# Attention outputs of two batches at once, and their products with W_out in seven: a two-layer graph attention kernel

## The chip, the cores and the metric

The kernel runs on one core of a Trainium2 chip. The metric is device time in microseconds, measured from outside the kernel; the median of three runs of the kernel before is 2986.15 us (2981.69 to 2986.96).

A core has five engines with instruction queues of their own: TensorE (PE; its weight loads are listed apart as PEld), VectorE (DVE), ScalarE (ACT), GpSimd (POOL) and SyncE (SP), which here only issues DMAs. Each engine works through its queue in order and waits on semaphores for the others. SBUF is the working memory, PSUM [...] is where TensorE writes.

## The reference

The input is x of 128 batches x 128 nodes x 512 features, fp32, and an adjacency mask of 128 x 128 per batch. Two layers follow each other. With LN the layer norm without scale and shift:

```
layer 0:  q, k, v = x Wq, x Wk, x Wv                 (4 heads of 64)
          P = softmax(where(adj, q k^T / 8, -max))
          h = LN(x + concat(P v) Wo + bo)
layer 1:  q, k, v = (LN(h) * gamma + beta) Wqkv^T    (8 heads of 64)
          P = softmax(where(adj | eye, q k^T / 8, -1e9))
          out = LN(h + concat(P v) Wout^T + b_out)
```

## The kernel before

All arithmetic is fp32. Two batches make a group (G = 2), so there are NG = 64 groups. The program is a software pipeline written out by hand: `step(s)` (L531) issues the work of several groups in a fixed order, and that order is the order of each engine's queue; nothing reorders it. In step s stand, among others, layer 0's q, k, v products of group s, layer 0's scores of group s - 1, layer 1's q and k products of group s - 2, and layer 1's scores and v products of group s - 3. A step has two halves, one for each batch of its groups (k = 2s and 2s + 1).

*Products in seven.* The q, k, v products take a group's two batches and two halves of the features as a 2 x 2 block matrix and form seven half-size products in place of eight (Winograd's form of Strassen's method). `sums` (L257, four additions on GpSimd at L266) makes the sums of the left side; the sums of the weights are made once. Products 1, 6, 7 and 4 accumulate one after the other in one PSUM bank ("a"), 5 and 3 in another ("f"), 2 in a third ("c"). After each product its bank is read, by ScalarE (1, 5, 6, 4) or by VectorE (2, 3, 7), before the next product of that bank may write. `product` (matmuls at L304; reads at L330, L332, L335) does so for layer 1, `product_0` (L361; L371, L373, L376) for layer 0. Below, "qk product 5" or "v product 4" are these.

*Attention.* `scores` (L386) multiplies q with k into rotating PSUM banks (pool ps_mm, five banks), GpSimd fills the target with the masked value (L410), VectorE copies the scores where the mask allows it (L412) and takes the row maximum (L415); for layer 1 it first joins the mask with the unit matrix (L407). ScalarE takes exponentials and their sums, one instruction per head (L424). `normalised` (L427) takes reciprocals on VectorE and multiplies on GpSimd (L433). To transpose the probabilities, `blocks` (L436) transposes 32 x 32 blocks on VectorE (L448), and two rounds of DMA through a scratch in HBM (`put` L198, `fetch` L204) move the blocks. `attend` (L458) multiplies them with v and ScalarE copies the result out (L474), batch by batch.

*Output and normalisation.* `residual` (L487) multiplies one batch's attention output with W_out, 512 columns at a time: two matmuls in layer 0, four in layer 1 (L493), each recorded as two instructions. VectorE adds the residual (L499), to which `addend` (L476) had added the bias on GpSimd (L484), and takes mean and variance (L501, L503); GpSimd forms the roots (L506 to L517); `norms` (L522) normalises on VectorE (L524), called later by `flush`. Layer 0's result h is then turned in the same way as the probabilities: `turn` (L208) transposes on VectorE (L214) and puts it, `arrive` (L219) fetches it, `finish` (L245) brings it in order on ScalarE and applies gamma and beta (L252), and `sums` follows. Layer 0's input x takes the same path through `in_order` (L235, ScalarE at L241). ScalarE rescales h (L483) to the residual of layer 1, since layer 1's norm is applied together with layer 0's.

SP issues every DMA in program order: loads (L72, L73), puts, fetches and outputs (L528).

Of the kernel before, what the change touches and what calls it, by code (L numbers as in the profile page):

```python
# [17 lines left out]
P = 128  # L18
# [9 lines left out]
def kernel(ctx: ExitStack, tc: tile.TileContext, x, adj, wq, wk, wv, wo, bo,  # L28
# [13 lines left out]
    four = ctx.enter_context(tc.tile_pool(name="four", bufs=4))  # L42
    dram = ctx.enter_context(tc.tile_pool(name="dram", bufs=2, space=bass.MemoryType.DRAM))
    ps_mm = ctx.enter_context(tc.tile_pool(name="ps_mm", bufs=5, space=PSUM))
# [9 lines left out]
    later, waiting = [], []  # L54
# [5 lines left out]
    def exponentials(left=0):  # L60
        while len(waiting) > left:
            waiting.pop(0)()


    X, M = {}, {}

    def load(g):
        if g >= NG:
            return
        X[g] = four.tile([P, G, E], F32, tag="x", name=f"x_{g}")  # L70
        M[g] = four.tile([P, G, N], U8, tag="m", bufs=6, name=f"m_{g}")
        nc.sync.dma_start(X[g], x[g * G:(g + 1) * G].rearrange("b n e -> n b e"))  # L72
        nc.sync.dma_start(M[g], adj[g * G:(g + 1) * G].rearrange("b i j -> i b j"))  # L73
# [8 lines left out]
    mhalf = const.tile([P, 2], F32, name="mhalf")  # L82
# [25 lines left out]

    spare = []
    for tag, n in (("qk1", 4), ("v1", 2), ("xT1", 2), ("xs1", 2)):  # L110
        rows_n = one.tile([P, n, E], F32, tag=tag, name=f"raw_{tag}")
        spare.extend(rows_n[:, i] for i in range(n))

    def load_transposed(dst, src, name, scaled=0):
        rows, cols = src.shape
        raws = []
        for r in range(rows // P):
            if not spare:
                raw = three.tile([P, cols], F32, tag="h", bufs=7, name=f"{name}_{r}")
            else:  # L120
                raw = spare.pop(0)
            nc.sync.dma_start(raw, src[r * P:(r + 1) * P, :])
            raws.append(raw)
# [36 lines left out]
    def weight_sums():  # L160
        for w, ws in ((w1qk, wsqk), (w1v, wsv)):
            for c in range(KH):
# [6 lines left out]
                t2, t3, t4 = ws[:, 0, c], ws[:, 1, c], ws[:, 2, c]  # L169
                nc.vector.tensor_sub(t3, b22, b12)  # L170
                nc.vector.tensor_sub(b12, b12, b11)
                nc.vector.tensor_sub(t2, b22, b12)
                nc.vector.tensor_sub(t4, b21, t2)

    def weight_sums_0():
        b11, b12, b21, b22 = (w0[:, c:c + KH, h].rearrange("p c t f -> p c (t f)")
                              for c in (0, KH) for h in range(2))
        t2, t3, t4 = (ws0[:, i].rearrange("p c t f -> p c (t f)") for i in range(3))
# [4 lines left out]

    weight_sums_0()
    load_transposed(w1, w_qkv, "w_qkv", scaled=INNER[1])
    setup.append(turn_gamma_beta)
    load_transposed(wo1, w_out, "w_out")
    setup.append(weight_sums)

    WO = (wo0, wo1)  # L190
    RATIO, H, XT, QK, V, QKV = {}, {}, {}, {}, {}, {}
# [14 lines left out]
    TURNED, SCR, RAW = {}, {}, {}  # L206

    def turn(l, g, b):  # L208
        if not 0 <= g < NG:
            return  # L210
        if b == 0:
            TURNED[l] = one.tile([P, 4, G * KC * 32], F32, tag=f"turned{l}", name=f"turned{l}_{g}")
        src = X[g][:, b] if l == 0 else H[g, b]
        nc.vector.transpose(TURNED[l].rearrange("p a (b c i) -> p a b c i", b=G, c=KC)[:, :, b],  # L214
                            src.rearrange("p (c a i) -> p a c i", a=4, i=32))
        if b == G - 1:
            SCR[l] = put(TURNED[l], f"scr{l}_{g}")

    def arrive(l, g):  # L219
        if not 0 <= g < NG:  # L220
            return
        RAW[l] = one.tile([P, 4, G, KC, 32], F32, tag=f"raw{l}", name=f"raw{l}_{g}")
        fetch(RAW[l].rearrange("p a b c i -> p a (b c i)"), SCR[l])

    def first_transposed():
        xT = XT[0, 0] = one.tile([P, KC, T], F32, tag="xT0", name="xT0_0")
        for b in range(G):
            pt = mm_tile(f"xt_{b}")
            for c in range(KC):
                nc.tensor.transpose(pt[:, c * N:(c + 1) * N], X[0][:, b, c * P:(c + 1) * P], ident)  # L230
# [26 lines left out]
    def sums(l, g):  # L257
        xT = XT[l, g]
        xs = one.tile([P, 4, KH, N], F32, tag=f"xs{l}", name=f"xs{l}_{g}")
        a = xT.rearrange("p (h c) (b n) -> p b h c n", h=2, b=2)  # L260
# [6 lines left out]
        XS[l, g] = xs  # L267
# [362 lines left out]
```

## Time and profile before

| What | Value |
|---|---|
| median of three runs | 2986.15 us (2981.69 to 2986.96) |
| the profiled execution | 2984.46 us |
| its span, first to last instruction | 2982.7 us |
| mean granted TensorE clock | 0.994 |
| TensorE busy | 2920.0 us (98%) |
| VectorE, ScalarE, GpSimd busy | 1854.0 (62%), 1334.2 (45%), 1567.4 us (53%) |
| DMA | 414 MB, 139 GB/s in the mean |
| W_out matmuls (L493) | 1536 instructions, 713.2 us busy |

The profile is of one execution. A line of the timeline gives start (from the span's start), length, engine, source line, operation, written tile <- read tiles, shapes and count; a bracket tells how long the engine idled before it and what ended that. The chain of waits is followed backwards from the last instruction: each piece is what its successor waited for. A busy share is a mean over the whole span and doesn't say whether an engine was late at the moment at which it was wanted.

### The profile page before, as it was taken

The numbers are of one execution on the slowest core, as the hardware profiler recorded it, in microseconds if no ns is written. First come the engines' busy times: TensorE is split into PE (matmuls) and PEld (weight loads), VectorE is DVE, ScalarE is ACT, GpSimd is POOL, SyncE is SP. The second block draws the span as 40 slices with busy tenths as digits, with TensorE's granted clock in tenths as the row PEclk, the third lists the DMA queues.
The fourth block names the chain that finished last, engine by engine and source line by source line (L and its number), as shares of the span: only waits on it lengthen the run. The fifth ranks groups of instructions, "written<-read, shape, count | busy, mean of one in ns | idle before, by whom it ended". The sixth has DMA issues, their size and how long they took to land.

```text
span 2982.7 us, 59421 instructions
## 1 busy us (share of the span) xinstructions
PE 2920.0 (98%) x22089; PEld 2402.9 (81%) x22089; DVE 1854.0 (62%) x3291; ACT 1334.2 (45%) x4619; POOL 1567.4 (53%) x2055
## 2 busy tenths in 40 slices
PE   6899999999999999999999999999999999999997
PEld 5788888888888888888888888888888888888865
DVE  4466666666666666666656666666666666666654
ACT  2344444444444444444544444444444444444442
POOL 2455545545545555555555555455455455455543
PEclk8999999999999999999999999999999999999999
DMA  5454544544544544544544545545445445445332
GB/s 170 123 149 129 150 141 127 161 136 124 165 135 125 165 136 127 160 134 134 156 132 140 150 131 147 146 129 153 141 126 161 137 122 168 133 125 163 118 100 89
DMA packets 249136, 414.42 MB, mean 139 GB/s; under 512 B 41608, under 2 KB 181392, under 8 KB 248848
## 3 DMA queue, kind: packets, MB, share of 16 engines
q1 hardware_dynamic: 248848, 410.62, 46.3%
q8 instruction: 175, 2.87, 0.4%
q14 instruction: 113, 0.93, 0.1%
HBM read 209.72 MB, written 200.80 MB: 138 GB/s over the span
## 4 chain that ended last, share of the span: by engine, by line
PE 96%; DVE 1%; DMA 1%; ACT 1%; issue 0%; POOL 0%; SPq 0%; POOLq 0%; DVEq 0%; ACTq 0%
PE o L493 22%; PE qka L304 15%; PE a L361 12%; PE qkf L304 8%; PE va L304 8%; PE sc L400 6%; PE av L471 6%; PE f L361 6%; PE qkc L304 4%; PE vf L304 4%; PE c L361 3%; PE vc L304 2%; ACT sm L424 1%; DMA scrp<-turned 0%; DMA pT<-scrp 0%
## 5 line engine op out<-in xcount | busy, mean ns | idle before, releaser
L424 ACT ACTIVATE sm<-sm,nmax 128x128 f32<-128x128 f32 x1536 | 595.2, 389 | 618.6 <-DVE nmax L415 604.9
L493 PE MATMUL o<-wo,aT 128*128 128x512 f32 x1536 | 713.2, 600 | 10.0 <-ACT aT L474 10.0
L506 POOL TENSOR_SCALAR ve<-mv 128x1 f32<-128x1 f32 x256 | 57.0, 223 | 1133.0 <-DVE rec L432 798.8
L493 PEld LDWEIGHTS o<-wo,aT 128*128 128x128 f32 x1536 | 278.3, 191 | 269.3 <-issue 246.8
L433 POOL TENSOR_TENSOR sm<-sm,rec 128x512 f32<-128x512 f32 (+1 forms) x256 | 397.0, 1561 | 171.9 <-DVE rec L432 171.9
L412 DVE COPY_PREDICATED sm<-m,sc 128x512 f32<-128x512 uint8 (+1 forms) x512 | 271.0, 581 | 29.1 <-POOL sm L410 7.0
L424 ACT ACTIVATION_READ_ACCUMULATOR sm<-sm,nmax 128x1 f32 x1536 | 288.0, 187 | 0.0
L448 DVE STREAM_TRANSPOSE turned<-sm 128x512 f32<-128x512 f32 (+1 forms) x256 | 246.0, 965 | 45.0 <-POOL sm L433 45.0
L304 PE MATMUL qkf<-xs,w 128*128 128x128 f32 x2048 | 249.9, 275 | 0.1
L304 PE MATMUL qka<-xs,wsqk 128*128 128x128 f32 x2048 | 249.6, 275 | 0.0
L415 DVE TENSOR_REDUCE nmax<-sm 128x4 f32<-128x512 f32 (+1 forms) x256 | 244.0, 953 | 8.8
L304 PEld LDWEIGHTS qkf<-xs,w 128*128 128x128 f32 x2048 | 239.0, 192 | 0.6 <-POOL xs L266 0.4
L304 PEld LDWEIGHTS qka<-xs,wsqk 128*128 128x128 f32 x2048 | 239.0, 192 | 0.0
L524 DVE TENSOR_SCALAR h<-h,mv,rstd 128x512 f32<-128x512 f32 x128 | 70.0, 547 | 265.0 <-POOL rstd L513 265.0
L432 DVE RECIPROCAL rec<-total 128x4 f32<-128x4 f32 (+1 forms) x256 | 44.7, 175 | 296.6 <-ACT sm L424 296.6
L266 POOL TENSOR_TENSOR xs<-xT 128x256 f32<-128x256 f32 x256 | 186.0, 727 | 34.4 <-PE w_qkvt L129 14.5
L410 POOL MEMSET sm<- 128x512 f32 (+1 forms) x256 | 181.1, 735 | 1.4 <-DVE turned L448 1.3
L330 ACT COPY ev<-va 128x256 f32<-128x256 f32 x128 | 47.6, 372 | 298.7 <-PE va L304 298.7
L513 POOL TENSOR_TENSOR rstd<-ve,mhalf 128x2 f32<-128x2 f32 (+1 forms) x256 | 165.9, 648 | 21.3
L330 ACT COPY eqk<-qka 128x512 f32<-128x512 f32 x128 | 75.1, 587 | 214.4 <-PE qka L304 214.4
L484 POOL TENSOR_TENSOR h<-h,bias 128x512 f32<-128x512 f32 x128 | 162.7, 1271 | 7.0 <-ACT h L483 6.9
L484 POOL TENSOR_TENSOR x<-x,bias 128x512 f32<-128x512 f32 x128 | 162.2, 1267 | 0.0
(122 smaller groups left out, 5825.5 us busy)
## 6 DMA issues: line engine op xcount, KB each, us to landing
scrp<-turned SPq DMA_DIRECT2D x124, 768.0 KB, 3.3
pT<-scrp SPq DMA_DIRECT2D x496, 192.0 KB, 4.0
scr<-turned SPq DMA_DIRECT2D x127, 512.0 KB, 2.7
raw<-scr SPq DMA_DIRECT2D x508, 128.0 KB, 3.0
x<-in_x_dram SPq DMA_DIRECT2D x64, 512.0 KB, 4.2
out_dram<-y SPq DMA_DIRECT2D x128, 256.0 KB, 2.0
m<-in_adj_dram SPq DMA_DIRECT2D x64, 32.0 KB, 4.0
scrp<-turned SPq DMA_DIRECT2D x4, 512.0 KB, 3.2
```

Source lines behind the costliest of these rows:

```text
L266: nc.gpsimd.tensor_tensor(o, a0, a1, op=op)
L304: nc.tensor.matmul(o, lhsT, rhs, start=first and n == 0, stop=n == len(todo) - 1, skip_group_check=True)
L361: nc.tensor.matmul(acc[:, t * P:(t + 1) * P], lhsT, rhs, start=first and n == 0, stop=n == len(todo) - 1, skip_group_check=True)
L400: nc.tensor.matmul(ps[h % 2][:, h // 2, :], q_, k_, start=True, stop=True)
L410: nc.gpsimd.memset(sm, (NEG0, NEG1)[l])
L412: nc.vector.copy_predicated(sm[:, s], mask[:, None, :].to_broadcast([P, K, N]), ps[s][:, :K, :])
L415: nc.vector.tensor_reduce(nmax, sm, AX.X, ALU.max, negate=True)
L424: nc.scalar.activation(sm[:, s, k, :], sm[:, s, k, :], AF.Exp, bias=nmax[:, s, k:k + 1], accum_out=total[:, s, k:k + 1])
L433: nc.gpsimd.tensor_tensor(sm, sm, rec[:, :, :, None].to_broadcast([P, 2, K, N]), op=ALU.mult)
L448: nc.vector.transpose(t[:, :, lo:hi, :], sm)
L484: nc.gpsimd.tensor_tensor(xin, xin, (bias0, bias1)[l], op=ALU.add)
L493: nc.tensor.matmul(pm, aT[:, c * P:(c + 1) * P], WO[l][:, c, :], start=(c == 0), stop=(c == nk - 1))
```

## The change

Layer 0's and layer 1's products with W_out are formed in seven for the two batches of a group, as the q, k, v products are; each product is added by VectorE straight from PSUM into its quarter of the residual R, which takes the place of x, h and y in one buffer of six. The left side's sums are four more GpSimd additions per layer (`out_sums`). `attend` runs once a step for both batches, one step later than before for layer 1. Means, roots and normalisations are made for both batches of a group; layer 1's normalisation moves from VectorE to ScalarE, output and load are one DMA each per group. The mask is joined with the unit matrix once per group. The rotating PSUM banks become four, and layer 0's second accumulating bank gets one of its own. `step` is written anew, with NG + 4 steps. In the first products of its second half, an output addition stands between the two layers' masks.

The core of the diff; the old bodies of the functions are shown above.

```diff
-    four = ctx.enter_context(tc.tile_pool(name="four", bufs=4))
+    six = ctx.enter_context(tc.tile_pool(name="six", bufs=6))
-    ps_mm = ctx.enter_context(tc.tile_pool(name="ps_mm", bufs=5, space=PSUM))
+    ps_mm = ctx.enter_context(tc.tile_pool(name="ps_mm", bufs=4, space=PSUM))
...
+    def turn(l, g):
+        if not 0 <= g < NG:
+            return
+        t = one.tile([P, 4, G * KC * 32], F32, tag="turned_in", name=f"turned{l}_{g}")
+        for b in range(G):
+            nc.vector.transpose(t.rearrange("p a (b c i) -> p a b c i", b=G, c=KC)[:, :, b],
+                                R[g][:, b].rearrange("p (c a i) -> p a c i", a=4, i=32))
+        SCR[l] = put(t, f"scr{l}_{g}")
+    def out_product(l, g, *which):
+        if not 0 <= g < NG:
+            return
+        aT, so = AT[l, g], SO[l, g]
+        hk = INNER[l] // P // 2
+        w, ws = WO[l], WSO[l]
+        EH = E // 2
+        for i in which:
+            left = {1: aT[:, 0, :hk], 2: aT[:, 0, hk:], 3: so[:, 3], 4: aT[:, 1, hk:], 5: so[:, 0],
+                    6: so[:, 1], 7: so[:, 2]}[i]
+            right = {1: w[:, :hk, :EH], 2: w[:, hk:, :EH], 3: w[:, hk:, EH:], 4: ws[:, 2],
+                     5: w[:, :hk, EH:], 6: ws[:, 0], 7: ws[:, 1]}[i]
+            bank, first = INTO[i]
+            if first and bank == "c":
+                ACC["o", bank] = mm_tile(f"oc{l}_{g}")
+            elif first:
+                ACC["o", bank] = ps_st.tile([P, 512], F32, tag=(bank, f"{bank}0")[l], name=f"o{bank}{l}_{g}")
+            acc = ACC["o", bank][:, :EH]
+            for c in range(hk):
+                nc.tensor.matmul(acc, left[:, c], right[:, c], start=first and c == 0, stop=c == hk - 1,
+                                 skip_group_check=True)
+            b, h = {1: (0, 0), 2: (0, 0), 6: (0, 1), 3: (0, 1), 5: (1, 1), 7: (1, 1), 4: (1, 0)}[i]
+            part = R[g][:, b, h * EH:(h + 1) * EH]
+            nc.vector.tensor_add(part, acc, part)
...
+    def with_self(g):
+        if 0 <= g < NG:
+            nc.vector.tensor_tensor(M[g], M[g], eye[:, None, :].to_broadcast([P, G, N]), op=ALU.max)
...
+    def attend(s):
+        for l, g in ((0, s - 2), (1, s - 4)):
+            if not 0 <= g < NG:
+                continue
+            K = HEADS[l] // 2
+            aT = AT[l, g] = one.tile([P, G, K, N], F32, tag=f"aT{l}", name=f"aT{l}_{g}")
+            for b in range(G):
+                pT = PT.pop((l, g, b))
+                if l == 1 or b == 0:
+                    pm = mm_tile(f"av{l}_{g}_{b}").rearrange("p (k n) -> p k n", n=N)
+                for h in range(HEADS[l]):
+                    i, kk = h % 2, h // 2
+                    o = pm[i * D:(i + 1) * D, (b * K if l == 0 else 0) + kk, :]
+                    v = (QKV[g][:, b, kk, 2, i * D:(i + 1) * D] if l == 0
+                         else V[1, g][:, b, h * D:(h + 1) * D])
+                    nc.tensor.matmul(o.rearrange("p (a r) -> p a r", r=32), v, pT[:, :, i * K + kk, :],
+                                     start=True, stop=True)
+                if l == 1:
+                    nc.scalar.copy(aT[:, b], pm)
+                elif b == G - 1:
+                    nc.scalar.copy(aT.rearrange("p b k n -> p (b k) n"), pm)
+    def out_sums(l, g):
+        if not 0 <= g < NG:
+            return
+        K = HEADS[l] // 2
+        so = SO[l, g] = one.tile([P, 4, K // 2, N], F32, tag=("so", "xs0")[l], name=f"so{l}_{g}")
+        halves_sums(so, AT[l, g].rearrange("p b (h c) n -> p b h c n", h=2))
+    def addend(l, g):
+        if not 0 <= g < NG:
+            return
+        if l == 1:
+            for b in range(G):
+                nc.scalar.activation(R[g][:, b], R[g][:, b], AF.Copy, scale=RATIO[g][:, b:b + 1])
+        nc.gpsimd.tensor_tensor(R[g], R[g], (bias0, bias1)[l][:, None, :].to_broadcast([P, G, E]),
+                                op=ALU.add)
+    def stats(l, g, b):
+        if not 0 <= g < NG:
+            return
+        if b == 0:
+            MV[l, g] = two.tile([P, G, nc.vector.BN_AGGR_DIM], F32, tag="mv", name=f"mv{l}_{g}")
+        st = three.tile([P, nc.vector.BN_STATS_DIM], F32, tag="st", name="st")
+        nc.vector.bn_stats(st, R[g][:, b])
+        nc.vector.bn_aggr(MV[l, g][:, b], st)
+        if b == G - 1:
+            roots(l, g)
+    def roots(l, g):
+        mv = MV[l, g]
+        n = 2 - l
+        ve = two.tile([P, 2, G], F32, tag="ve", name=f"ve{l}_{g}")
+        nc.gpsimd.tensor_scalar_add(ve[:, 0], mv[:, :, 1], EPS)
+        if l == 0:
+            nc.gpsimd.tensor_scalar(ve[:, 1], mv[:, :, 1], 1.0 + EPS, EPS * EPS, op0=ALU.mult,
+                                    op1=ALU.add)
+        root = two.tile([P, 2, G], F32, tag="root", name=f"root{l}_{g}")
+        nc.gpsimd.tensor_tensor(root[:, :n].rearrange("p i b -> p (i b)"),
+                                ve[:, :n].rearrange("p i b -> p (i b)"), mhalf[:, :n * G], op=ALU.pow)
+        if l == 0:
+            ratio = RATIO[g] = three.tile([P, G], F32, tag="ratio", bufs=5, name=f"ratio_{g}")
+            nc.gpsimd.tensor_tensor(ratio, ve[:, 1], root[:, 1], op=ALU.mult)
+            nc.gpsimd.tensor_tensor(ratio, ratio, root[:, 0], op=ALU.mult)
+            later.append(lambda: norms_0(g, mv, root))
+        else:
+            shift = two.tile([P, G], F32, tag="shift", name=f"shift_{g}")
+            nc.gpsimd.tensor_tensor(shift, mv[:, :, 0], root[:, 0], op=ALU.mult)
+            nc.gpsimd.tensor_scalar_mul(shift, shift, -1.0)
+            later.append(lambda: norms_1(g, shift, root))
+    def norms_0(g, mv, root):
+        for b in range(G):
+            nc.vector.tensor_scalar(R[g][:, b], R[g][:, b], mv[:, b, 0:1], root[:, 1, b:b + 1],
+                                    op0=ALU.subtract, op1=ALU.mult)
+    def norms_1(g, shift, root):
+        for b in range(G):
+            nc.scalar.activation(R[g][:, b], R[g][:, b], AF.Identity, bias=shift[:, b:b + 1],
+                                 scale=root[:, 0, b:b + 1])
+        nc.sync.dma_start(out[g * G:(g + 1) * G].rearrange("b n e -> n b e"), R[g])
...
+        k = 2 * s
+        if s:
+            load(s + 1)
+        made = scores(k)
+        masked(made, 0)
+        masked(made, 1)
+        exps(0, k)
+        addend(0, s - 2)
+        with_self(s - 2)
+        p("qk", 4, g=s - 3)
+        product_0(s, 1)
+        attend(s)
+        exps(1, k)
+        out_sums(0, s - 2)
+        product_0(s, 5)
+        p("", g=-1)
+        product_0(s, 2)
+        addend(1, s - 4)
+        p("", g=-1)
+        out_product(0, s - 2, 1, 5, 2)
+        normalised(k)
+        out_product(0, s - 2, 6)
+        product_0(s, 6)
+        p("", g=-1)
+        out_product(0, s - 2, 3)
+        stats(0, s - 2, 0)
+        out_product(0, s - 2, 7)
+        product_0(s, 3)
+        p("", g=-1)
+        out_product(0, s - 2, 4)
+        product_0(s, 7)
+        stats(0, s - 2, 1)
+        p("v", 1, 5, g=s - 3)
+        blocks(k)
+        product_0(s, 4)
+        p("v", 2, g=s - 3)
+        flush()
+        turn(1, s - 2)
+        arrive(1, s - 2)
+        probs_arrive(k)
+        k += 1
+        made = scores(k)
+        masked(made, 0)
+        p("v", 6, g=s - 3)
+        out_sums(1, s - 4)
+        out_product(1, s - 4, 1)
+        exps(0, k)
+        masked(made, 1)
+        p("v", 3, g=s - 3)
+        exps(1, k)
+        out_product(1, s - 4, 5, 2)
+        p("v", 7, g=s - 3)
+        out_product(1, s - 4, 6)
+        p("v", 4, g=s - 3)
+        normalised(k)
+        finish(s - 2)
+        turn(0, s + 1)
+        blocks(k)
+        out_product(1, s - 4, 3)
+        stats(1, s - 4, 0)
+        out_product(1, s - 4, 7)
+        arrive(0, s + 1)
+        probs_arrive(k)
+        p("qk", 1)
+        p("qk", 5)
+        out_product(1, s - 4, 4)
+        stats(1, s - 4, 1)
+        p("qk", 2)
+        p("qk", 6)
+        in_order(s + 1)
+        flush()
+        p("qk", 3, 7)
     first_transposed()
-    for s in range(NG + 3):
+    for s in range(NG + 4):
         step(s)
```

## The prediction

> **What bounds the kernel now.** I read the page first, then the chain of waits over one step, then VectorE, ScalarE and GpSimd in the same stretch. Page and chain:
>
> ```profile
> span 2982.7 us, 59421 instructions
> PE 2920.0 (98%) x22089; PEld 2402.9 (81%) x22089; DVE 1854.0 (62%) x3291; ACT 1334.2 (45%) x4619; POOL 1567.4 (53%) x2055
> ```
> ```profile
> 1454.99 1.54 PE sc L400 x24
> 1456.53 3.63 PE o L493 x8
> ...
> 1470.43 1.72 PE o L493 x4
> 1472.15 0.86 PE va L304 x4
> ...
> 1478.01 1.06 PE va L304 x4
> 1479.07 3.43 PE o L493 x8
> ...
> 1486.36 1.72 PE o L493 x4
> ...
> 1498.35 1.79 PE qka L304 x16
> 1500.14 1.54 PE sc L400 x24
> ```
>
> The chain is TensorE alone. A step (two batches) lasts 1500.14 - 1454.99 = 45.15 us, and 60 full steps run from 145.6 to 2854. The other 2982.7 - 60 x 45.15 = 274 us are filling and draining. The output products take 3.63 + 1.72 + 3.43 + 1.72 = 10.50 us of a step; the rest takes 34.65. A pass of 512 columns costs 3.43/8 = 0.429 us, one of 256 costs 0.86/4 = 0.216. Going to or from the 64-row score matmuls costs about 0.2 (va: 1.06 instead of 0.86).
>
> VectorE around the second half's scores, then one GpSimd and one ScalarE line:
>
> ```profile
> 1475.23 0.55 DVE L524 TENSOR_SCALAR h<-h,mv,rstd 128x512 f32<-128x512 f32 x1 [1.40 <-POOL rstd L513]
> 1475.81 0.71 DVE L214 STREAM_TRANSPOSE turned<-h 128x512 f32<-128x512 f32 x1
> 1476.44 0.39 DVE L335 TENSOR_TENSOR v<-vc,ev 128x256 f32<-128x256 f32 x1
> 1476.75 0.41 DVE L335 TENSOR_TENSOR v<-vf,ev 128x256 f32<-128x256 f32 x1
> 1477.21 0.78 DVE L412 COPY_PREDICATED sm<-m,sc 128x256 f32<-128x256 uint8 x2
> 1478.02 0.69 DVE L415 TENSOR_REDUCE nmax<-sm 128x4 f32<-128x512 f32 x1
> ...
> 1479.04 1.34 DVE L412 COPY_PREDICATED sm<-m,sc 128x512 f32<-128x512 uint8 x2
> 1480.41 1.22 DVE L415 TENSOR_REDUCE nmax<-sm 128x8 f32<-128x1024 f32 x1
> ...
> 1485.18 1.25 DVE L524 TENSOR_SCALAR y<-y,mv,rstd 128x512 f32<-128x512 f32 x1
> ```
> ```profile
> 1485.11 3.08 POOL L433 TENSOR_TENSOR sm<-sm,rec 128x512 f32<-128x512 f32 x2
> ```
> ```profile
> 1486.44 2.07 ACT L252 ACTIVATE xT<-raw,gb 128x256 f32<-128x256 f32 x4
> ```
>
> VectorE runs in order; start to start gives what each costs the queue: 0.31 for a 256-wide addition from PSUM, 0.81 + 0.61 and 1.37 + 1.14 for the two layers' masks and maxima, 0.63 for a transpose. It keeps up now because the second half of a step (from 1476.47) has room: only one normalising and one turning stand there ahead of the scores.
>
> [...] here 256 columns from PSUM last 0.41, 512 last 0.69, so splitting costs. [...] the trace agrees (1.25 at 1485.18 behind a GpSimd multiplication, 0.51 when ahead of one). [...] the change puts products 1, 6, 7, 4 into one bank, each after VectorE has read the last.
>
> **The change, part by part, per step.**
> *Output products.* 24 passes of 512 become 42 of 256: 14 in layer 0, 28 in layer 1. 42 x 0.216 = 9.07, saving 1.43. One visit to the attention outputs instead of two saves one switch (0.2), and scores are now followed by short products that pay it. TensorE without waits: 34.65 + 9.05 = 43.7 us.
> *VectorE.* Four 512-wide additions (4 x 0.69) go, 14 of 256 (14 x 0.41 = 5.7) come; two scalings (2 x 0.89) move to ScalarE at 0.73; a mask operation of two goes. Net +1 us, about 30 of 44: not full, but see below.
> *GpSimd.* Eight half sums more: four of 256 (4 x 0.73), four of 128, which the trace lacks; the line through 0.73 (256) and 1.27 (512) gives 0.46, bounds 0.37 (half of 0.73) and 0.73. Bias additions of 1024 by the same line: 2.4, bounds 2.1 (the 1024 multiplication) and 2 x 1.27. Power over four values: 0.58 (one), 0.72 (two), so 1.0; bounds 0.72 and 1.44. Net about +3, under 28 of 44.
> *Moved.* The bringing in order of the next group's xT (L241, two copies, then four sums at L266) goes behind layer 1's qk product 6: copies end 1.8 before the step does, the sums 1.4 into the next, and the two memsets queued behind them on GpSimd (0.52 + 0.95) make the first masks 1.0 late. Covered: the exponentials that follow are wanted only behind the attention outputs at 8.5; without that cover it would be 1.0 a step. The two scalings now on ScalarE (1.4) run at the step's end under qk products 3 and 7 (3.6). The mask operation (0.28 before, 0.28 to 0.56 now) stands where VectorE idles until layer 0's q, k, v product 2. Layer 0's normalising and turning now come together, both batches, on VectorE right behind the last addition of v (product 2) and ahead of the second scores. On SP the put (L198) and four fetches (L204) move with them, past no slow wait; in before put to last landing is 8.2 to 9.8 us behind other transfers, 2.7 + 1.3 + 2.8 = 6.8 without, which I take. Output and load are one DMA each per group, hidden: the load, issued at a step's head, lands in 4.2 after the output's 2 and is turned 30 us later. Four rotating PSUM banks instead of five: the last score bank waits for that v addition, 0.1.
>
> *The walk.* Hand-overs cost about 0.1 (layer 0's f ends at 1470.43 on the chain, its addition starts at 1470.54). TensorE in the new order: scores 1.54, qk product 4 1.99, attention 3.12, seven layer 0 q, k, v products 7 x 1.34, seven output products 7 x 0.43, v's products 1, 5 and 2 3 x 0.86: their end is 21.6 after the step's start. On the way layer 0's output product 4 waits for output product 7's addition, queued behind the first batch's statistics (0.69 + 0.18): output product 3 ends at 14.3, its addition, the statistics and that addition at 16.1, TensorE is ready at 15.9: wait 0.3. GpSimd: ScalarE rescales the residual behind the eight exponentials (until 13.3: attention copies end at 8.5, exponentials 3.09, one copy, two rescalings), then bias 2.4, multiplications 1.04 + 2.08 to 18.9, roots to 21: just in time.
>
> Now from that end (V): VectorE v addition to +0.4; two normalisings 0.92, plus 0.5 for GpSimd's sums (bounds 0 and 1.5, two whole 0.73 sums), +1.8; two transposes +3.1; layer 0 masks and maxima +4.5; one output addition +4.8; layer 1 masks and maxima, maxima ready +7.4; three additions +8.2; v product 7's addition +8.65. TensorE wants v product 4, same bank, at 1.54 + 0.2 + 7 x 0.86 = +7.76: it gets it at +8.75, and all behind it waits 1.0.
> Behind that addition stand on VectorE product 6's addition, the reciprocals, two transposes of x and those of the probabilities; none of these is wanted by TensorE before qk product 5.
> ScalarE: eight exponentials 3.09 (eight took 1462.46 to 1465.55 in before) from +7.5, v copy, four xT activations (L252): the second chunk at +11.95, the last +12.95. GpSimd sum +13.75. So layer 1's qk product 5, due at +12.13, starts at +13.85: 1.7 late, the wait of 1.0 included. What is late next: layer 1's output product 4 waits for product 7's addition, behind transposes of probabilities (GpSimd done +13.0), product 3's addition and statistics: +16.0 against +15.65: 0.35.
>
> Sum: 43.7 + 0.3 + 1.7 + 0.35 = 46.1 us, 0.9 over before. 60 x 46.1 = 2766. Filling and draining: one more step (layer 1's attention a step later), but no attention in the second step; 274 becomes 280 (260 to 300). Span 3046. The profiled execution took 1.8 more than its span and the median is 1.7 above it: **3050 us**.
>
> **Rivals.**
> *A, faster: TensorE stays the bound.* The chain v addition, masks, exponentials, xT, sum fits into TensorE's 12.1 us up to product 5 or nearly. For it: no engine's busy time is near 44. Against it: its parts sum to 13.85 even when nothing collides (13.35). It decides once waits are under 1.35 a step ((2983 - 280)/60 = 45.05). With 0.5 of waits: 60 x 44.2 + 280 + 4 = 2936; with none 2906.
> *B, slower still, one collision fully paid.* Both normalisings wait for a GpSimd sum each (+1.0), or the fetch takes 9.8 as before behind the probabilities' put instead of 6.8: it lands at +13 where ScalarE wants it at +10.9 (+2). 47.1 to 48.1: 3110 to 3170.
> *C, saving and waits cancel:* 45.05, 2980 to 2992.
> *D, the change doesn't do what it says:* 14 short groups each lose 0.1 at their head and the saving is gone. Against: va, vf, vc, equally short, follow each other at 0.86.
>
> **How the numbers follow.** Likeliest 0.52: 45.6 to 46.9, 3020 to 3098, its own range. A 0.24, spread from 2906 to 2980; B 0.18, from 3098 to 3170; C (with D) 0.06. Range 2945 to 3120: 0.1 of A and 0.1 of B stay outside. Measurement tells 0.2%, 6 us. Faster 0.24, same 0.06, slower 0.70.
>
> **What would show it.** The distance between steps on the chain, 46.1; va L308 waiting for VectorE once a step, near 1 us; qkf waiting for GpSimd's or qka for ScalarE's xT; VectorE normalisings longer than 0.55; TensorE busy share under 96%; output passes at 0.216. Wrong if the step is 44 with no wait on va, if the fetch decides, or if a pass of 256 costs more than 0.22.

## The result and the profile after

| | before | after |
|---|---|---|
| median of four runs, us | 2984.86 (2981.69 to 2986.96) | 3069.73 (3068.78 to 3070.35) |
| span of the profiled execution, us | 2982.7 | 3066.9 |
| one full step, us: median (mean of 60) | 45.14 (45.15) | 46.02 (46.05) |
| filling and draining, us: span less 60 mean steps | 274 | 304 |

The kernel before has one run more here than above, so its median differs a little. The changed kernel is slower: the ratio is 1.0285, with a 95% interval of 1.0267 to 1.0303. The medians stand 2.8 us above the span here and 2.2 us before. First the head of the page of the changed kernel:

```profile
span 3066.9 us, 62670 instructions
PE 2925.4 (95%) x23241; PEld 2645.0 (86%) x23241; DVE 1896.0 (62%) x3747; ACT 1432.8 (47%) x4683; POOL 1721.3 (56%) x2247
```

TensorE's share fell from 98% to 95%, and no other engine is near full: what grew is idle time of TensorE. Its busy time did not fall, although the output products do less work. Busy time hides waits here: in one full step TensorE counts as busy for 45.14 of 46.02 us, while the starts below show 2.29 us of waits. Most of these lie inside the records: q, k product 1 is given as 2.32 us below, where the kernel before has 1.95. Starts are the better measure, and they are used from here on. The chain of waits over one step, columns start, length, what:

```profile
1493.68 1.54 PE sc L428 x24
...
1509.54 0.70 PE oa L400 x2
...
1515.61 0.14 DVE v L339
...
1515.95 1.56 DVE r L577 x2
...
1520.44 1.27 DVE sm L446 x2
...
1523.95 0.34 DVE v L339
...
1524.33 1.13 PE va L308 x4
...
1539.70 1.54 PE sc L428 x24
```

Before, this chain held TensorE only. Now it leaves TensorE at 1515.6, behind v product 2, runs 8.7 us over VectorE (normalising, turning, masks, maxima, the additions of v and of the output) and comes back at v product 4. A step lasts 1539.70 - 1493.68 = 46.02 us. The same stretch in TensorE's own queue (start, length, line, operation; in brackets the idle time before it and what ended it):

```profile
1522.46 1.03 PE L400 MATMUL oa<-wso,so 128*128 128x256 f32 x4
1524.33 1.13 PE L308 MATMUL va<-wsv,xT 128*128 128x256 f32 x4 [0.85 <-DVE v L339]
...
1526.16 1.03 PE L400 MATMUL oa<-wso,so 128*128 128x256 f32 x4
1527.07 2.32 PE L308 MATMUL qka<-xT,w 128*128 128x128 f32 x16
1529.35 2.05 PE L308 MATMUL qkf<-xs,w 128*128 128x128 f32 x16
1531.43 1.13 PE L400 MATMUL oa<-wso,aT 128*128 128x256 f32 x4
1532.40 1.95 PE L308 MATMUL qkc<-xT,w 128*128 128x128 f32 x16
```

Start to start, four passes of 256 without a wait take 0.86 and a q, k product 1.79. The differences are the waits of a step: v product 4 comes 1524.33 - 1522.46 - 0.86 = 1.0 late and the product behind it another 0.10, the start of q, k product 1 another 0.04, product 5 is 2.28 - 1.79 = 0.49 late, output product 4 is 2.08 - 1.79 = 0.29 late and what follows it 0.10. Layer 0's output product 4 adds 0.27 (its 0.70 on the chain instead of 0.43). Together 2.29, so that TensorE without these waits takes 46.02 - 2.29 = 43.73 us a step. Both halves of the prediction's sum are there: the work saved, and the larger waits that came instead.

VectorE and GpSimd in the same stretch:

```profile
1515.95 1.56 DVE L577 TENSOR_SCALAR r<-r,mv,root 128x512 f32<-128x512 f32 x2
1517.44 1.29 DVE L219 STREAM_TRANSPOSE turned<-r 128x512 f32<-128x512 f32 x2
```
```profile
1515.15 0.53 POOL L444 MEMSET sm<- 128x512 f32 x1
1515.64 0.73 POOL L271 TENSOR_TENSOR so<-aT 128x256 f32<-128x256 f32 x1
1516.45 0.79 POOL L271 TENSOR_TENSOR so<-so,aT 128x256 f32<-128x256 f32 x1
...
1518.73 0.96 POOL L444 MEMSET sm<- 128x1024 f32 x1
```

The two normalisings hold VectorE for 1517.44 - 1515.95 = 1.49 us, 0.57 more than the 0.92 at which the prediction had put two of them. The kernel before shows how far one can differ: 1.25 us behind a GpSimd multiplication (at 1485.18), and 0.51 ahead of one, where the next instruction starts 1466.23 - 1465.80 = 0.43 us later:

```profile
1465.80 0.51 DVE L524 TENSOR_SCALAR y<-y,mv,rstd 128x512 f32<-128x512 f32 x1
1466.23 1.30 DVE L214 STREAM_TRANSPOSE turned<-x 128x512 f32<-128x512 f32 x2
```
```profile
1465.97 2.10 POOL L433 TENSOR_TENSOR sm<-sm,rec 128x1024 f32<-128x1024 f32 x1 [2.16 <-DVE rec L432]
```

In the changed kernel GpSimd's first filling ends at 1515.15 + 0.53 = 1515.68, before they start, and its second comes behind them; what runs beside them is sums.

### The profile page after: what moved, and what is told of

It is laid out like the page before. It is cut to its first block, busy times and chain, and to the rows that moved or that the text cites. A ratio compares the mean times of both kernels' runs of the same rounds, so it can differ in the third digit from the quotient of the medians.

```text
span 3066.9 us, 62670 instructions
## 1 busy us (share of the span) xinstructions
PE 2925.4 (95%) x23241; PEld 2645.0 (86%) x23241; DVE 1896.0 (62%) x3747; ACT 1432.8 (47%) x4683; POOL 1721.3 (56%) x2247
## 4 chain that ended last, share of the span: by engine, by line
PE 76%; DVE 15%; issue 5%; DMA 2%; ACT 1%; POOL 1%; SPq 0%; ACTq 0%; DVEq 0%; POOLq 0%
PE qka L308 16%; PE a L364 11%; PE oa L400 8%; PE qkf L308 8%; PE f L364 6%; PE av L513 6%; DVE sm L446 4%; PE va L308 4%; PE qkc L308 4%; PE of L400 3%; DVE r L577 3%; PE sc L428 3%; PE c L364 3%; DVE r L404 2%; PE vc L308 2%
## 5 line engine op out<-in xcount | busy, mean ns | idle before, releaser
L471 POOL TENSOR_TENSOR sm<-sm,rec 128x512 f32<-128x512 f32 (+1 forms) x256 | 373.6, 1470 | 401.2 <-DVE rec L470 401.2
L534 POOL TENSOR_TENSOR r<-r,bias 128x1024 f32<-128x1024 f32 x128 | 302.4, 2362 | 282.3 <-ACT r L533 282.3
L404 DVE TENSOR_TENSOR r<-oa,r 128x256 f32<-128x256 f32 x512 | 211.2, 413 | 102.0 <-PE oa L400 87.4
L486 DVE STREAM_TRANSPOSE turned<-sm 128x512 f32<-128x512 f32 (+1 forms) x256 | 239.5, 954 | 32.8 <-POOL sm L471 32.8
L400 PE MATMUL oa<-wso,so 128*128 128x256 f32 x768 | 213.9, 388 | 4.1 <-DVE r L404 4.1
L400 PE MATMUL of<-wo,so 128*128 128x256 f32 x768 | 209.5, 382 | 4.9 <-POOL so L271 4.9
L271 POOL TENSOR_TENSOR so<-aT 128x128 f32<-128x128 f32 (+1 forms) x256 | 151.9, 593 | 109.8 <-ACT aT L518 109.8
L378 DVE TENSOR_TENSOR qkv<-c,e 128x384 f32<-128x384 f32 x64 | 35.7, 557 | 264.1 <-PE c L364 260.5
L545 DVE BATCH_NORM_STATS2 st<-r 128x6 f32<-128x512 f32 x256 | 177.2, 692 | 6.7
L400 PEld LDWEIGHTS oa<-wso,so 128*128 128x128 f32 x768 | 141.6, 191 | 35.7 <-issue 18.7
```

What stands on the lines that cost most here:

```text
L271: nc.gpsimd.tensor_tensor(o, a0, a1, op=op)
L400: nc.tensor.matmul(acc, left[:, c], right[:, c], start=first and c == 0, stop=c == hk - 1, skip_group_check=True)
L404: nc.vector.tensor_add(part, acc, part)
L471: nc.gpsimd.tensor_tensor(sm, sm, rec[:, :, :, None].to_broadcast([P, 2, K, N]), op=ALU.mult)
L486: nc.vector.transpose(t[:, :, lo:hi, :], sm)
L534: nc.gpsimd.tensor_tensor(R[g], R[g], (bias0, bias1)[l][:, None, :].to_broadcast([P, G, E]), op=ALU.add)
```

## The experiments

The step given with each is the median distance between the starts of layer 1's q, k product 4 on TensorE; in each kernel 48 to 58 of the 60 full steps lie within 0.1 us of it. The theory: the path from v product 2 over VectorE to v product 4, and on over the exponentials and xT to q, k product 1, became longer than what TensorE has to do meanwhile. The main rivals: the visible wait of v product 4 is the loss in itself; or TensorE got slower through its short groups.

### Away with the visible wait alone

```diff
         p("v", 7, g=s - 3)
         out_product(1, s - 4, 6)
-        p("v", 4, g=s - 3)
         normalised(k)
-        finish(s - 2)
         turn(0, s + 1)
         blocks(k)
         out_product(1, s - 4, 3)
         stats(1, s - 4, 0)
         out_product(1, s - 4, 7)
         arrive(0, s + 1)
         probs_arrive(k)
+        p("v", 4, g=s - 3)
+        finish(s - 2)
```

> The changed kernel, but on TensorE v product 4 stands behind layer 1's output products 3 and 7, and its copy and xT follow it; VectorE's order is untouched. Theory (the chain v addition, normalisings, turning, masks and maxima, exponentials, xT, sum sets the step; the wait on va is only where it shows first): the wait of va for VectorE goes, but its copy and so xT come later: step 46.0 to 46.6 us, time 3070 to 3105. Rival (the 1.0 us that TensorE waits on va is itself the loss): step 45.0, time about 3010.

Measured: 3087.39 us, ratio 1.0343 (1.0313 to 1.0373), step 46.3. The wait at v product 4 went, and a longer one came at q, k product 1. TensorE's waits in the full steps, summed (who waits, for whom: us in total, times, longest):

```profile
PE qka L308 <- ACT xT L256: 55.0, 57, 1.1
```

But part of this new wait is of the edit's own making. The copy of v product 4 stands ahead of xT in ScalarE's queue and comes later with that product:

```profile
1536.25 0.37 ACT L336 COPY v<-va 128x256 f32<-128x256 f32 x1 [0.50 <-PE va L308]
1536.52 2.08 ACT L256 ACTIVATE xT<-raw,gb 128x256 f32<-128x256 f32 x4
```

ScalarE idles for 0.50 us between the exponentials and this copy; q, k product 1 waits 0.96 in this step. So the run shows that v product 4 cannot be put off at no cost, and does not decide between theory and rival. The runs that shorten the path decide that.

### The normalising left out

```diff
     def norms_0(g, mv, root):
         for b in range(G):
-            nc.vector.tensor_scalar(R[g][:, b], R[g][:, b], mv[:, b, 0:1], root[:, 1, b:b + 1],
-                                    op0=ALU.subtract, op1=ALU.mult)
+            pass
```

> The changed kernel without layer 0's normalisation on VectorE (h goes on unnormalised, so the output is another). Theory: 1.5 us less on VectorE ahead of the second masks, so masks, exponentials and xT come 1.5 earlier; the waits of 1.0 (va) and 0.5 (xT) go, the wait of layer 1's output product 4 grows from 0.3 to about 0.6: step 44.4 to 44.9, time 2975 to 3000. Rival (the order and shape of TensorE's own work is what costs, its waits are small change): step 45.7 to 46.0, time over 3050.

Layer 0's normalising is left out here, and nothing else. Measured: 3019.89 us, ratio 1.0117 (1.0087 to 1.0146), step 45.25. The gain of 50 us lies in the direction of the theory and rules its rival out, but it is 0.35 to 0.85 us a step short of what the theory had asked for. VectorE shows why:

```profile
1495.71 0.42 DVE L404 TENSOR_TENSOR r<-oa,r 128x256 f32<-128x256 f32 x1 [0.57 <-PE oa L400]
1496.08 1.34 DVE L446 COPY_PREDICATED sm<-m,sc 128x512 f32<-128x512 uint8 x2
```

Once VectorE is early, it stands idle for 0.57 us for layer 1's output product 1, whose addition was put ahead of layer 1's masks. This second path was hidden behind the first and ends close behind it; the walk of the prediction had followed only the one that ended last.

### GpSimd's sums of layer 1 left out

```diff
-                left = {1: aT[:, 0, :hk], 2: aT[:, 0, hk:], 3: so[:, 3], ...}[i]
+                left = aT[:, int(i in (4, 5, 7)), :hk] if i in (1, 3, 5) else aT[:, int(i in (4, 5, 7)), hk:]
...
         p("v", 6, g=s - 3)
-        out_sums(1, s - 4)
```

> The changed kernel without layer 1's left sums of the output products (plain halves of the attention output are multiplied instead, so the output is another); GpSimd has nothing but two memsets while VectorE normalises. Theory with the collision: the two normalisings fall from 1.5 to between 0.9 (a memset doesn't block) and 1.25 (it does), step 45.4 to 45.8, time 3035 to 3058. Rival (collisions with GpSimd cost nothing on the path): 46.0, 3070.

The four half sums of layer 1's attention outputs are left out; the products run on as many columns of other data. Measured: 3047.72 us, ratio 1.0210 (1.0180 to 1.0239), step 45.8. The normalisings, and all that GpSimd does beside them (its filling of both score tiles):

```profile
1509.84 1.33 DVE L581 TENSOR_SCALAR r<-r,mv,root 128x512 f32<-128x512 f32 x2
1511.09 1.29 DVE L219 STREAM_TRANSPOSE turned<-r 128x512 f32<-128x512 f32 x2
```
```profile
1509.03 1.42 POOL L448 MEMSET sm<- 128x512 f32 x2
```

They hold VectorE for 1.25 us now instead of 1.49, but not for 0.92. The 0.33 that is left comes with the filling, and this filling is new in this place: in the changed kernel the second one starts at 1518.73 (above), behind the normalisings, and without the sums it moves up beside them. So the run puts one collision in the place of another, and its 0.24 us are the least that the sums cost; by the timeline of the changed kernel, where nothing but sums runs beside the normalisings, they cost 0.57. The sums do not explain the whole loss: without them the step is still 0.65 above the kernel before.

### The masks of both layers together again

```diff
         masked(made, 0)
+        masked(made, 1)
         p("v", 6, g=s - 3)
         out_sums(1, s - 4)
         out_product(1, s - 4, 1)
         exps(0, k)
-        masked(made, 1)
```

> Undoes one part of the change: in a step's second half the two layers' masks stand together on VectorE, and output product 1's addition behind them. Theory: layer 1's maxima come 0.33 earlier and so do exponentials and xT: step 45.7, time about 3050; output product 6 now waits about 0.8 for that addition, and v product 4 starts when it did. Rival (the addition between the masks keeps TensorE going, its wait is what counts): step 46.5 to 47, time 3100 and more.

Measured: 3056.91 us, ratio 1.0241 (1.0211 to 1.0270), step 45.8. With the masks together and the filling ahead of the sums, 12.8 us of the 85 are gone (3069.73 - 3056.91). Their place does not decide while the normalising stands ahead: most of the wait moved from v product 4, now 0.37 late, to output product 6, 0.82 late, which shares its bank with product 1 (`PE oa` waits 37.2 us in 57 steps for `DVE r`). The second filling now runs beside the normalisings.

### The order of the q, k products

```diff
         p("qk", 1)
-        p("qk", 5)
+        p("qk", 2)
         out_product(1, s - 4, 4)
         stats(1, s - 4, 1)
-        p("qk", 2)
+        p("qk", 5)
         p("qk", 6)
```

> Only the order of layer 1's q, k products is changed: 1, 2, output product 4, 5, 6 instead of 1, 5, output product 4, 2, 6. In the changed kernel product 5 starts 0.49 us late a step (the half sum of xT) and output product 4 0.29 plus about 0.1 of a restart. Theory (these waits are the end of the same chain that starts at v product 2): product 2 needs xT but no half sum, so both waits are covered by its 1.79 us; the step falls from 46.02 to 45.15 to 45.35, 3010 to 3030 us. Rival (the waits are only moved, to product 2, since the last piece of xT comes 2.07 us after the first): step 45.7 or more, 3048 us or more.

Measured: 3069.37 us, ratio 1.0280 (1.0265 to 1.0295), step 46.0: nothing gained. The order of TensorE's starts:

```profile
1479.95 2.32 PE L308 MATMUL qka<-xT,w 128*128 128x128 f32 x16
1482.11 1.95 PE L308 MATMUL qkc<-xT,w 128*128 128x128 f32 x16
1484.25 1.13 PE L400 MATMUL oa<-wso,aT 128*128 128x256 f32 x4 [0.19 <-DVE r L404]
```

Product 1 still takes 1482.11 - 1479.95 = 2.16, so 0.37 of the 0.49 lies in product 1 itself, which needs the second piece of xT; only 0.12 was product 5's wait for the half sum. And output product 4 comes 2.14 - 1.79 = 0.35 late, as before, since product 7's addition is late whichever product stands ahead of it. The rival holds here: these waits are ends of the late path, and an exchange among its ends gains nothing.

### The normalising on ScalarE

```diff
         if l == 0:
+            shift = two.tile([P, G], F32, tag="shift0", name=f"shift0_{g}")
+            nc.gpsimd.tensor_tensor(shift, mv[:, :, 0], root[:, 1], op=ALU.mult)
+            nc.gpsimd.tensor_scalar_mul(shift, shift, -1.0)
...
-            nc.vector.tensor_scalar(R[g][:, b], R[g][:, b], mv[:, b, 0:1], root[:, 1, b:b + 1],
-                                    op0=ALU.subtract, op1=ALU.mult)
+            nc.scalar.activation(R[g][:, b], R[g][:, b], AF.Identity, bias=shift[:, b:b + 1],
+                                 scale=root[:, 1, b:b + 1])
...
-        stats(0, s - 2, 0)
         out_product(0, s - 2, 7)
+        stats(0, s - 2, 0)
```

> The order of e5, and layer 0's normalising done by ScalarE (shift prepared by GpSimd) instead of VectorE, and the first batch's statistics of layer 0 behind output product 7's addition. Theory: TensorE without waits is 43.72 a step, and with normalising off VectorE only the wait of v product 4 in e2 (0.24 plus 0.1) is left, since the layer-1 masks stand behind output product 1's addition: step 44.0 to 44.3, 2940 to 2970 us, faster than the kernel before. Rival (TensorE itself got slower through its short groups, so that its floor is near 45): 2990 us or more.

Measured: 3034.18 us, ratio 1.0162 (1.0145 to 1.0179), step 45.5. The theory's range is missed by 64 us. By the total alone the rival would hold, but the trace contradicts its reason: TensorE's starts show the same 43.7 us of work and 1.7 us of waits. The exchange of the statistics took away the 0.27 of layer 0's output product 4; v product 4 still waits 0.72. VectorE and GpSimd show a third thing that had been hidden:

```profile
1503.04 0.42 DVE L404 TENSOR_TENSOR r<-oa,r 128x256 f32<-128x256 f32 x1 [0.28 <-PE oa L400]
1503.89 1.35 DVE L446 COPY_PREDICATED sm<-m,sc 128x512 f32<-128x512 uint8 x2 [0.43 <-POOL sm L444]
```
```profile
1502.91 0.95 POOL L444 MEMSET sm<- 128x1024 f32 x1
```

With the masks apart, the filling of layer 1's score tile is issued behind the four sums on GpSimd and ends at 1503.86. The masks start at once behind it.

### The filling first, then the masks too

The first kernel issues that filling ahead of the sums and leaves the masks where the change put them:

```diff
+        filled(made, 0)
+        filled(made, 1)
         masked(made, 0)
         p("v", 6, g=s - 3)
         out_sums(1, s - 4)
         out_product(1, s - 4, 1)
         exps(0, k)
         masked(made, 1)
```

where `filled` holds the `memset` that `masked` had.

> As e6, with GpSimd's filling of layer 1's score tile (0.95 us) ahead of the four sums of layer 1's attention outputs instead of behind them; the masks stay behind output product 1's addition. In e6 VectorE waited 0.43 us for this filling, and 0.28 for output product 1. Theory (both stand between v product 2 and v product 7's addition, and each counts): step 45.46 to 45.0, 3000 to 3012 us. Rival A (the filling is all that parts e6 from e7): step 44.2 to 44.4, 2958 to 2972. Rival B (the filling does not count, since product 1 is waited for anyway): 3030 to 3036.

Measured: 2996.71 us, ratio 1.0040 (1.0025 to 1.0055), step 44.9: the theory's direction and size, 3 us better than its range. The second kernel moves the masks as well, and the filling with them:

```diff
         masked(made, 0)
+        masked(made, 1)
         p("v", 6, g=s - 3)
         out_sums(1, s - 4)
         out_product(1, s - 4, 1)
         exps(0, k)
-        masked(made, 1)
```

> As e6, and layer 1's masks ahead of output product 1's addition, as in the kernel before. Theory: v product 7's addition ends at about +7.5 after v product 2, before TensorE wants v product 4 at +7.76, so no wait is left but the 0.2 behind the scores: step 43.7 to 44.0, 2922 to 2950 us. Rival (output product 6, which needs product 1's addition in the same bank, waits instead, as it did by 0.65 in e4): no faster than e6.

Measured: 2960.63 us, ratio 0.9916 (0.9901 to 0.9931), step 44.2. It is faster than both kernels, but 11 us above the theory's range. TensorE is busy for 97% of the span again. One of its steps:

```profile
1206.71 1.03 PE L400 MATMUL oa<-wso,so 128*128 128x256 f32 x4
1207.57 1.03 PE L308 MATMUL va<-wsv,xT 128*128 128x256 f32 x4
...
1209.30 1.03 PE L400 MATMUL oa<-wso,so 128*128 128x256 f32 x4
1210.16 1.97 PE L308 MATMUL qka<-xT,w 128*128 128x128 f32 x16
1211.97 1.95 PE L308 MATMUL qkc<-xT,w 128*128 128x128 f32 x16
1214.16 1.13 PE L400 MATMUL oa<-wso,aT 128*128 128x256 f32 x4 [0.24 <-DVE r L404]
```

v product 4 and q, k product 1 follow without a gap. What is left is the wait of output product 4, 2.19 - 1.79 = 0.40 here, for product 7's addition. TensorE's waits in the full steps, summed, and ScalarE in one of the few steps in which xT still comes late:

```profile
PE oa L400 <- DVE r L404: 8.7, 38, 0.3
PE qka L308 <- ACT xT L256: 3.8, 7, 0.9
```
```profile
1475.42 2.08 ACT L256 ACTIVATE xT<-raw,gb 128x256 f32<-128x256 f32 x4 [0.67 <-DMA raw<-scr]
```

There ScalarE waits for the fetch, which has become a limit in some steps, but not in most.

The place of masks and filling was worth 0.2 us a step with the normalising on VectorE (46.0 to 45.8), and 1.3 without it (45.5 to 44.2, of which the filling takes 0.6 and the masks 0.7).

### What stands in filling and draining

The prediction gave 280 us to filling and draining; it is 304. Layer 1's first q, k product 4 comes at 103.9 before and at 115.6 after; from the last one to the end it is 42.9 us before and 58.9 after. Two guesses on the filling were tried, first the weight sums:

```diff
         combine(*(w[:, c:c + hk, h * E // 2:(h + 1) * E // 2] for c in (0, hk) for h in range(2)),
-                *(WSO[l][:, i] for i in range(3)))
+                *(WSO[l][:, i] for i in range(3))) if False else nc.gpsimd.memset(WSO[l], 0.01)
```

> The changed kernel without the combining of the output weights: the eight VectorE additions that make the sums of w_out for the seven products are left out, and their place is filled by GpSimd (the output is another). They stand in the filling, at 43.84 to 46.90 and 52.46 to 56.10, ahead of the first masks and of layer 0's products. Theory (filling and draining cost 30 us more than before, and these 6.7 us are part of the 12 more in filling): the first product 4 of layer 1 comes at 109 to 112 instead of 115.6, the total falls by 4 to 7 us, 3062 to 3066. Rival (the fill waits for loads and round trips of the probabilities anyway): unchanged within 1.5 us.

Measured: 3065.70 us, ratio 1.0273 (1.0256 to 1.0290), and the first product 4 at 114.8. The total lies in the theory's range, the mark that it named does not: 0.8 us earlier instead of 4 to 7. Kernels whose filling was not touched have this mark between 114.6 (e2) and 116.6 (e3), so that even the 0.8 says little. Nearly all of those 6.7 us are hidden, as the rival says; of the 3.6 us by which the profiled span is shorter, 2.2 lie between the first and the last product 4, where nothing was changed, and that the total fits is luck. The second guess:

```diff
         probs_arrive(k)
+        if s < 2:
+            turn(0, s + 1)
+            arrive(0, s + 1)
         k += 1
...
-        turn(0, s + 1)
+        if s >= 2:
+            turn(0, s + 1)
         blocks(k)
...
-        arrive(0, s + 1)
+        if s >= 2:
+            arrive(0, s + 1)
```

> The changed kernel, but in its first two steps the turning of the next group's x with its put and fetch stands ahead of the second half's scores, as in the kernel before, and not behind their masks, exponentials and reciprocals; all later steps are as changed. Theory (the moved bringing in has its cover only in full steps; in the filling it lies open: there the chain goes scores, masks, exponentials, turning, put 2.69, fetch 3.17 to 3.5, xT 1.15, sums, and TensorE waits 19.4 us for xT in two steps): the first product 4 of layer 1 comes at 104 to 110 instead of 115.6, the total is 5 to 11 us less, 3059 to 3065. Rival (another chain of the filling ends nearly as late): first product 4 at 114 or later, 3067 to 3070.

Measured: 3064.84 us, ratio 1.0268 (1.0253 to 1.0284), first product 4 at 115.3. Again the mark fails and the total fits by luck: of the 4.3 us by which the profiled span is shorter, 3.1 lie between the first and the last product 4. TensorE's waits for x between 40 and 120 us, first of the changed kernel, then of this one:

```profile
PE a L364 <- ACT xT L245: 19.4, 2, 12.3
```
```profile
PE a L364 <- ACT xT L245: 16.4, 2, 11.1
```

In its chain of waits the put of the turned x now stands behind the put and the fetches of the probabilities in SP's queue, and is issued at 63.36 instead of 64.22. One delay took the other's place. In the kernel before no wait of `PE a` for xT appears in this stretch. That points to when x is brought in, but no run shows it, and which edit makes the 12 us stays open.

> e7 with the first two steps of e10. Theory: the two do not touch each other, so the gain of e10 comes on top of e7's 2960.6: 2950 to 2956. Rival: as e7.

Both together: 2957.37 us, ratio 0.9909 (0.9893 to 0.9926). This is 3 us under e7 and above the theory's range, and the intervals of the two ratios overlap: that the two gains add up is not shown.

The drain was not tried apart. Its chain of waits shows these pieces, first of the changed kernel's end, then of the kernel before:

```profile
3042.24 1.99 PE av L513 x16
...
3044.84 1.24 ACT r L533 x2
...
3046.15 2.34 POOL r L534
3048.49 0.70 POOL so L271
...
3049.23 2.07 PE of L400 x4
```
```profile
2968.27 1.99 PE av L471 x16
...
2970.98 5.17 PE o L493 x8
```

After the last attention the rescaling, the bias for both batches and a sum lie bare on the path, and the seven products follow with their additions between them. From the last attention to the end it takes 3066.9 - 3042.2 = 24.7 us; before it was 2982.7 - 2968.3 = 14.4. That is 10 of the 16 us; where the other 6 lie was not followed up.

## Why the prediction was right

The forecast was 3050 us and slower; 3069.7 is inside its range and the likeliest case's own. The mechanism was right too: the path from v product 2 over VectorE to v product 4 and q, k product 5 sets the step, and the runs that shorten it gain. Step by step:

- *TensorE without waits, 43.7.* Measured 43.73. A pass of 256 in the output products costs 0.86/4 = 0.216 as it did in the v products; rival D, that short groups lose 0.1 each, falls, except where a group follows a wait (0.10 each). The 43.73 still hold the 0.20 of the last score bank (below), which the prediction had not put into its sum; the bare work is 43.5, so the agreement is in part luck.
- *v product 4 at +8.75 instead of +7.76.* Product 2 ended at 1515.52 (1514.64 + 0.88 on the chain), so it started 8.81 behind that end, and 1.0 late. The normalisings' collision with GpSimd's sums was estimated at 0.5 and measured 0.57.
- *q, k product 5 1.7 late in all.* Measured 1.00 + 0.10 + 0.04 + 0.49 = 1.63. Product 5 started at 1529.35, +13.83, against +13.85 in the walk. The walk charged its lateness to the half sum alone. The sum did end last, but e5 shows that 0.37 of the 0.49 would stay without it: they lie in product 1, at the second piece of xT, for which the walk had a time and no wait.
- *Output products 4: 0.3 in layer 0, 0.35 in layer 1.* Measured 0.27, and 0.29 with 0.10 behind it.
- *The last score bank, 0.1.* Measured 0.20: v product 6 starts 1.74 behind the second scores' start, 1.54 before.
- *The sum of a step, 46.1.* Measured 46.02, in the mean 46.05.
- *The fetch in 6.8.* Put at 1518.76, the last piece landed at 1525.68, in 6.9, ahead of ScalarE's xT at 1526.41. It did not decide. It had little to spare: over the whole span ScalarE waits for it 3 times here and 22 times in e7, 15.6 us in all there.
- *Filling and draining, 280 (260 to 300).* This term was mis-sized and lies outside its own range: 304. It makes 24 us, and the mean step, 0.05 under the forecast, takes 3 of them back; the 21 us between the forecast span of 3046 and 3066.9 are this. "One more step, but no attention in the second step" counted whole steps, and not what lies bare when no TensorE work is there to cover it: rescaling, bias and a sum in the drain. In the filling TensorE waits 19.4 us for x, for a cause that stays open.

Rival A had the right mechanism for another kernel: e7 shows that with the path cut TensorE is the bound again and that the saving is real. It was wrong for this one, since the parts of the path did sum to more than TensorE's work. Of rival B's two causes one was there in a smaller size: the collision took 0.57 us, not the 1.5 of a whole sum for each normalising. The fetch did not decide.

## What to carry to other kernels

Cutting 1.4 us of matmul from a step pays only if every path that runs beside TensorE still fits into the shorter time: sum the path from the last product that feeds it to the first product that needs it, on each engine's queue in order, and compare. Then sum the second-longest too, because removing the longest gains only the distance between them; here three causes (the normalising, the filling's place, the masks' place) stood in one another's shadow. Masks and filling alone gained 13 us and the normalising alone (with the two reorderings of e6) 36; all together turned 3070 into 2961 us. A wait that the profile names can be no more than the place where a late path meets TensorE: the exchange of the waiting products in e5 gained nothing, and a shorter path did.

## What the runs showed that was not expected

- *Two normalisings took longer beside a filling as well.* It only writes, and still with nothing but GpSimd's two fillings beside them (e3) two normalisings held VectorE for 1.25 us instead of 0.92. With fillings and sums (e4) they held it for 1.67, from 1511.58 to 1513.25. In e3 the loss was smaller than what was left of the fillings: the first normalising started at 1509.84, the fillings ended at 1509.03 + 1.42 = 1510.45, so 0.61 us of them were left and 0.33 was lost. One pair in the changed kernel, ahead of its full steps, shows the two cases side by side: the first normalising (at 134.68) held VectorE for 0.81 us beside a filling that ended at 135.29, the second (at 135.49), with nothing of GpSimd beside it, for 0.45. The times on GpSimd are rough, and whether part of a normalising runs beside the filling is not shown.
- *TensorE's granted clock was lower in both drains.* It is 1.00 over a full step (1493.68 to 1539.70; before, 1454.99 to 1500.14). Two stretches of the changed kernel's drain (columns: stretch, its length, busy time and instructions of PE, PEld, DVE, ACT and POOL, granted clock, DMA share, GB/s): TensorE is busy for 3.98 of 7 us, the granted clock is 0.50, and it is 0.57 while the next products run.

```profile
3042.00:3049.00 7.00, 3.98 (x20) 2.78 (x20) 0.42 (x1) 2.21 (x4) 2.85 (x2) 0.50 0.20 75
3049.00:3055.00 6.00, 5.77 (x16) 4.66 (x16) 1.27 (x3) 0.00 (x0) 2.31 (x4) 0.57 0.01 3
```

  Four passes of 256 took 2.07 us there (at 3049.23, behind 3.01 us without work), where four take 0.86 in a full step. The kernel before shows the like: TensorE waited 4.88 us up to 2968.27, the granted clock was 0.50 from 2968 to 2971, and the last eight passes of 512 took 5.17 us (at 2970.98) instead of 3.43, at 0.71 in the mean. In both the lower clock came with waits of TensorE; no run shows what sets it. The forecast of the drain had left that out.
- *A group behind a wait took longer.* In the changed kernel a TensorE group that follows a wait for another engine takes 0.10 us more until the next one (0.97 instead of 0.86 behind v product 4 and behind output product 4), and e7, which has no wait at v product 4, has 0.86 behind it.
